# The attention-value product of every first query half in float16, each operand in two parts

## The chip, the cores and the metric

The kernel runs on one core of a Trainium2 chip. Five engines work side by side, each through its own queue in order: PE (matrix products, with a separate row PEld for loading the stationary operand), DVE (vector), ACT (activation), POOL (general purpose) and SP (here a queue that only issues transfers; ACT issues some too). They wait for each other by semaphores. Operands lie in SBUF, 128 partitions wide; matrix products write to PSUM. The metric is the time of one execution on the device in microseconds (us), and the median over runs is compared.

## The reference, cut to what matters

The program is one layer of gated attention and a feed-forward part, for four sequences of 512 tokens and 512 channels. The attention has a self branch and a cross branch; each has 8 groups of 2 query heads that share one key head and one value head, all 128 wide.

```python
ln_out = _ln(hidden_states, ln_w, ln_b)
q = _ln(_fp8_linear_pertensor(ln_out, wq, ...).reshape(b, s, g, hpg, d), qln_w, qln_b)
k = _ln(_fp8_linear_pertensor(ln_out, wk, ...).reshape(b, s, g, d), kln_w, kln_b)
v = _fp8_linear_pertensor(ln_out, wv, ...).reshape(b, s, g, d)
scores = jnp.einsum('bsghd,btgd->bghst', q, k) / np.sqrt(d)
core = jnp.einsum('bghst,btgd->bsghd', jax.nn.softmax(scores, axis=-1), v)
...
# the same once more with keys and values from ctx_2048 (no fp8 there): xout
catq = _div_clamp_fp8(jnp.concatenate([core, xout], axis=-1), proj_smooth)
out = jnp.einsum('bsi,oi->bso', catq, wproj) * (proj_in_scale * proj_w_scale)
```

`_div_clamp_fp8` rounds to 8-bit floating point, so a small error ahead of it can move a value by a whole step. That is why the products ahead of it are carried with more than 16 bits: either in float32, or as sums of float16 products, where a number x is held as a high part (x rounded to float16) and a low part (x minus the high part, rounded again). The feed-forward part after it (ternary weights, activations rounded to 8 bits) is not touched by the change.

## The kernel before, in words

**Tiling.** A block is one (branch, group, sequence): 64 blocks, first the 32 of the self branch, then the 32 of the cross branch. A block has two heads, and so two units of work; the main loop makes one step per unit, 128 steps. A unit's 512 queries are done in two halves of 256, h = 0 and h = 1. `half(n)` numbers all halves through, n = 2s + h for step s. The loop is followed by a stage that projects the attention's result and by the feed-forward stage.

**One half on PE.** `step` (line 805) is written as two passes, h = 0 and h = 1, and in each of them PE gets, in this order:

- `scores` of half n: 8 products of 256 columns into the PSUM tile `ps_s` (2 buffers)
- `shift_mm` of half n-1: 4 products of 256 columns, which subtract each query's largest score
- `pv` of half n-2 (line 668): the attention-value product, tile `po`, one buffer. 8 products of float32, 128 x 128 with 129 columns (the 129th column is of ones and yields the softmax's denominator). The page counts two PE records for each of them, 16 per half
- `top_turn` of half n: 2 small transposes of the running maxima into `mt`
- `mm` of a later block's token tile: the projections to queries, keys and values, tile `ps_p`, one buffer for each of the two token tiles of a pair. In the self branch 8 products of 256 columns and 16 of 128; in the cross branch 20 of 256
- `shift_row` of half n: 2 small products that lay the maxima out in a row, again `mt`

**Around it.** DVE makes `top` (tile `mx`, the maximum over `ps_s`), then for the projected tile of two halves ago `out` (line 564: `y`, `yj` with an accumulator, and `z`, the key's last step), `var`'s first half (line 554, tile `ss`, 128 x 3), then `nm` (the maximum over `mt`), and `evac` (line 682: the reciprocal `r` and two multiplications `ob`). ACT copies the row of maxima into `qk` (`shift_put`), writes `z` for the two query heads, squares the projected tile with a sum (`jk`), takes the exponential `pt` (line 665, 128 x 1024 float32) and copies the values to `vv`. POOL does `var`'s power, 128 x 3, which ends with the reciprocal square root.

**Once a step, in the pass h = 0.** `split` (line 579) makes the float16 parts of the queries and keys of a pair of token tiles: POOL adds a column to `z` (line 581), ACT casts the high part `hl` (128 x 768), POOL casts one more part (line 585) and subtracts for the low part (line 586), and SP issues a transposing transfer to `qk`. `quant` (line 694) rounds a unit's output to 8 bits on DVE in three passes over `ob`, 128 x 512; then SP issues a transposing transfer to `ot`, and ACT stores the `ot` of the unit before to DRAM, `cat_d`.

**In the background.** The weights of later groups are prepared piecemeal (`prep_w`, line 450: a sum `ms` and three multiplications `wf` on DVE, a cast `wq` on ACT and its low part on DVE, or POOL for some groups), as are the tokens of later sequences (`prep_self`, line 321) and the cross branch's context. A plan says at which point of which step each piece is put into the queues.

**What sets the order.** Instructions on PE, DVE and ACT go through `Ordered` (line 74). Where its switch is on, the order in the text is kept; elsewhere a scheduler orders them when the program is built. It is on from step 19 (`"p0"`, line 60) to three steps before the loop's end. POOL's and SP's instructions are not held to the text's order.

## Time and profile before

| what | value |
|---|---|
| median of 3 runs (lowest to highest) | 1761.45 us (1759.91 to 1762.43) |
| the profiled execution's own time | 1761.26 us |
| its span, first to last instruction | 1759.5 us |
| mean granted PE clock | 0.985 |
| busy share of the span | PE 95%, DVE 75%, ACT 60%, POOL 32% |
| start of the maxima in step 0 and step 19 | 61.9 us and 324.1 us |
| from one step to the next, steps 20 to 52 | 10.17 to 10.18 us |
| from one step to the next, steps 61 to 122 | 11.01 us |

The span is what lies between the first and the last instruction; the execution's own time is 1.8 us longer. Busy time is given for each engine; an engine can be busy all the time and still not be at its best rate, since the ends of PE's products are modelled. "Idle before" is what an engine waited ahead of an instruction, with the releaser that ended it. The chain that ended last is read backwards from the end: at each step to what released an instruction, or to its predecessor on its engine. A view in order of time gives start, duration, engine, line, operation and tiles (output first). Line 86 is the line in `Ordered` through which most instructions go, so here groups are told apart by tiles.

### The profile page before, as it was taken

Reading aid. Unit: us, or ns where it says so; the run is one execution under the profiler, and the core shown is the slowest. Engines: PE = TensorE matmul, PEld = TensorE weight load, DVE = VectorE, ACT = ScalarE, POOL = GpSimd, SP = SyncE. Lnnn points to the kernel's source line nnn. Section 1 sums busy time; section 2 is a strip of 40 time slices with the busy share of each in tenths; the row PEclk is TensorE's granted clock in tenths of the full one; section 3 lists DMA queues with packets and bytes.
Section 4 is the critical chain, followed back from the end, with each engine's and each line's share of the span. In section 5 each row is a group of like instructions: output and inputs, shape, how many; then the busy total and the mean of one; then the engine's idle time right before and its main releaser. Section 6 shows DMA issues by size and latency. Waiting matters only on the chain.

```text
span 1759.5 us, 40972 instructions
## 1 busy us (share of the span) xinstructions
PE 1672.0 (95%) x15174; PEld 1422.4 (81%) x15174; DVE 1324.2 (75%) x3967; ACT 1052.5 (60%) x3413; POOL 569.0 (32%) x725
## 2 busy tenths in 40 slices
PE   3589888999999999999999999999999999999999
PEld 2478787999999999999999999999999987443444
DVE  7888877777777778777777777777766665679876
ACT  6655555666666667666666666666665553457443
POOL 3453333334444335543333333333333330110000
PEclk8699999999999999999999999999999999999999
DMA  4433434344544455644445544544476664984333
GB/s 149 118 67 67 85 68 86 67 89 83 97 86 83 87 91 136 142 85 103 103 103 103 109 103 109 103 109 103 91 127 115 138 130 134 290 251 114 84 72 90
DMA packets 450312, 192.25 MB, mean 109 GB/s; under 512 B 417312, under 2 KB 421440, under 8 KB 447680
## 3 DMA queue, kind: packets, MB, share of 16 engines
q1 hardware_dynamic: 366688, 141.38, 38.7%
q10 hardware_dynamic: 82992, 44.07, 9.2%
q0 software_dynamic: 432, 4.19, 1.3%
q8 instruction: 119, 1.95, 0.4%
q14 instruction: 81, 0.66, 0.1%
HBM read 84.71 MB, written 23.09 MB: 61 GB/s over the span
## 4 chain that ended last, share of the span: by engine, by line
PE 82%; DVE 9%; ACT 3%; POOL 2%; DMA 2%; issue 1%; ACTq 0%; SPq 0%; DVEq 0%; POOLq 0%
PE ps_p L86 26%; PE po L86 23%; PE ps_s L86 17%; PE psj L86 5%; PE psd L86 3%; PE mt L86 3%; PE ub L86 3%; PE ga L86 3%; DVE mx L86 1%; DVE yb L86 1%; POOL ss L559 1%; DVE ob L86 1%; ACT z L86 1%; DMA ot<-ob 1%; DVE z L86 1%
## 5 line engine op out<-in xcount | busy, mean ns | idle before, releaser
L86 PE MATMUL ps_p<-wq,xa 128*128 128x256 f16 (+1 forms) x5584 | 557.5, 256 | 21.1 <-DVE xa L86 9.5
L86 PEld LDWEIGHTS <-xa 128*128 128x128 f16 x5632 | 471.7, 99 | 65.4 <-DVE xa L86 12.1
L86 PE MATMUL po<-vv,pt 128*128 128x129 f32 x4096 | 501.9, 275 | 0.0
L86 DVE TENSOR_REDUCE mx<-ps_s 128x256 f16<-128x1024 f32 x256 | 313.2, 1224 | 246.3 <-PE ps_s L86 244.9
L86 PEld LDWEIGHTS po<-vv,pt 128*128 128x128 f32 x4096 | 478.5, 192 | 4.0 <-PE ps_s L86 0.7
L86 PE MATMUL ps_s<-qk 128*128 128x256 f16 x3072 | 386.1, 274 | 14.8 <-ACT qk L86 8.0
L559 POOL TENSOR_TENSOR ss<-ss,mhalf 128x3 f32<-128x3 f32 x256 | 221.2, 864 | 497.2 <-DVE ss L86 490.1
L86 ACT CAST qk<-mt 1x256 f16<-1x256 f32 x256 | 92.4, 361 | 431.1 <-PE mt L86 422.0
L86 PEld LDWEIGHTS <-qk 128*128 128x128 f16 x3072 | 291.0, 98 | 49.1 <-issue 10.5
L86 ACT ACTIVATE pt<-ps_s 128x1024 f32<-128x1024 f32 x256 | 256.4, 1001 | 21.0 <-PE ps_s L86 20.3
L586 POOL TENSOR_TENSOR hl<-z,hl 128x768 f16<-128x768 f32 x126 | 207.4, 1646 | 19.6 <-ACT hl L86 19.6
L86 ACT ACTIVATE jk<-ps_p 128x128 f32<-128x128 f32 x762 | 192.3, 253 | 22.5 <-PE ps_p L86 19.1
L86 ACT ACTIVATE z<-ps_p,ss 128x127 f32<-128x127 f32 x508 | 154.4, 350 | 51.3 <-POOL ss L559 51.1
L86 DVE SCALAR_TENSOR_TENSOR ob<-po,r,rsr 128x128 bf16<-128x128 f32 x512 | 155.9, 346 | 7.7
L86 ACT ACTIVATION_READ_ACCUMULATOR jk<-ps_p 128x1 f32 x762 | 142.9, 188 | 0.0
L581 POOL TENSOR_TENSOR z<-acc,cb 128x2 f32<-128x2 f32 x128 | 27.2, 213 | 337.0 <-DVE ss L86 293.3
L86 DVE TENSOR_REDUCE nm<-mt 128x2 f16<-128x256 f16 x256 | 107.4, 419 | 29.4 <-PE mt L86 29.3
L86 DVE TENSOR_SCALAR ob<-ob 128x512 bf16<-128x512 bf16 (+2 forms) x384 | 111.9, 291 | 8.3
L86 ACT CAST hl<-z 128x768 f16<-128x768 f32 x128 | 105.8, 827 | 19.3 <-POOL z L581 17.1
L86 DVE SCALAR_TENSOR_TENSOR y<-ps_p,ss,gk 128x128 f32<-128x128 f32 x254 | 87.1, 343 | 28.8 <-ACT z L86 27.9
L86 PEld LDWEIGHTS <-nt 128*128 128x128 bf16 x512 | 50.0, 98 | 65.4 <-issue 6.2
L86 PE MATMUL psj<-wp,cat 128*128 128x512 f16 x448 | 97.0, 379 | 0.0
(149 smaller groups left out, 1773.8 us busy)
## 6 DMA issues: line engine op xcount, KB each, us to landing
cat_d<-ot ACTq DMA_DIRECT2D x128, 128.0 KB, 2.0
cat<-cat_d SPq DMA_DIRECT2D x16, 1024.0 KB, 5.6
wf<-in_dram ACTq DMA_DIRECT2D x56, 256.0 KB, 4.3
wt<-in_dram ACTq DMA_DIRECT2D x48, 256.0 KB, 4.3
wt<-in_dram SPq DMA_DIRECT2D x24, 512.0 KB, 4.4
xt<-in_dram SPq DMA_DIRECT2D x32, 256.0 KB, 4.4
cf<-in_dram SPq DMA_DIRECT2D x16, 256.0 KB, 3.6
out_dram<-o SPq DMA_DIRECT2D x16, 256.0 KB, 2.0
```

What stands on the lines that cost most here:

```text
L86: ins = f(*args, **kw)
L559: gp.tensor_tensor(ss[:, 2], ss[:, 1], mhalf[:, 0], ALU.pow)
L581: gp.tensor_tensor(z[:, :, 2, 0:1], self.acc, cb[:, self.ty : self.ty + 1].broadcast_to((128, 2, 1)), ALU.add)
L586: (low or gp).tensor_tensor(hl[:, :, 3:6], z, hl[:, :, 0:3], ALU.subtract)
```

## The change

- **The product.** For h = 0, `exps` writes the exponentials to a float32 tile `e` (one buffer). A new `high` on ACT casts it to float16 into the first half of the place where `pt` was, and a new `low` on DVE writes `e` minus that, in float16, into the second half. `pv` then takes three float16 products (high x high, high x low, low x high) in place of each float32 product: 24 products of 129 columns in place of 8. For h = 1 nothing is changed in the product but a bias in the exponential; `pt` and `vv` stay float32.
- **The values.** `vals` scales by 1/8; a new `vals16`, once a step, makes the two float16 parts of the values on POOL: a cast and a subtraction, 128 x 256 each.
- **The key's last step.** DVE's third instruction in `out` goes. A new `keys`, once a step, does it on POOL: a copy of one column, two instructions of 128 x 256 (subtract that column, add `hk`), and then the two small POOL instructions that `split` had. The rest of `split` becomes `high` and `low` of the pair.
- **The variance.** Its first half moves from DVE to POOL, two POOL instructions in place of one on each engine; a factor goes into constants.
- **The output's rounding.** `ob` belongs to a block, so `quant` runs once in two steps over 128 x 1024; one transposing transfer of twice the size in place of two, and two stores one step later. `quant` now stands at the end of the pass h = 0, behind `evac`.
- **Order.** POOL's instructions go through `Ordered` too, the switch is on from step 16, one background point moves from the end of a step to the middle of its pass h = 1, the weights' pieces come at three yields in four, and the scale tile `rsr` is loaded in 8 parts, not 4.

```diff
-    "p0": 19,
+    "p0": 16,
...
-    v, sc, pe = [Ordered(tc, e) for e in (nc.vector, nc.scalar, nc.tensor)]
-    gp, sy = nc.gpsimd, nc.sync
+    v, sc, pe, gp = [Ordered(tc, e) for e in (nc.vector, nc.scalar, nc.tensor, nc.gpsimd)]
+    sy = nc.sync
...
             def var(self, i):
                 ss = self.ss[:, i]
-                v.scalar_tensor_tensor(
-                    ss[:, 1], ss[:, 0], 1.0 / 128, epsv[:, self.ty, 0], ALU.mult, ALU.add
+                gp.tensor_tensor(ss[:, 1], ss[:, 0], epsv[:, self.ty], ALU.add)
+                gp.tensor_tensor(ss[:, 2], ss[:, 1], mhalf[:, 0], ALU.pow)
+
+            def vals(self, i):
+                sc.activation(
+                    self.v[:, self.pr * 2 + i, 0:128], self.ps[i][:, 384:512], AF.Copy, scale=V_SCALE
                 )
-                gp.tensor_tensor(ss[:, 2], ss[:, 1], mhalf[:, 0], ALU.pow)
-
-            def vals(self, i):
-                sc.copy(self.v[:, self.pr * 2 + i, 0:128], self.ps[i][:, 384:512])
+
+            def vals16(self):
+                tk = slice(self.pr * 2, self.pr * 2 + 2)
+                v32, vh, vl = self.v[:, tk, 0:128], self.v16[:, 0, tk, 0:128], self.v16[:, 1, tk, 0:128]
+                gp.tensor_copy(vh, v32)
+                gp.tensor_tensor(vl, v32, vh, ALU.subtract)
...
-                v.scalar_tensor_tensor(y, k, r[:, 2:3], gk[:, ty], ALU.mult, ALU.mult)
+                v.scalar_tensor_tensor(z[:, 2], k, r[:, 2:3], gk[:, ty], ALU.mult, ALU.mult)
...
-                v.scalar_tensor_tensor(z[:, 2], y, y[:, 0:1], hk[:, ty], ALU.subtract, ALU.add)
-
-            def split(self, low=None):
+
+            def keys(self):
                 z, hl = self.z, hl_tiles[self.k % 2]
+                k, y0 = z[:, :, 2], sm.tile([128, 2, 1], F32, name="y0", bufs=2)
+                gp.tensor_copy(y0, z[:, :, 2, 0:1])
+                gp.tensor_tensor(k, k, y0.broadcast_to((128, 2, 128)), ALU.subtract)
+                gp.tensor_tensor(k, k, hk[:, self.ty : self.ty + 1].broadcast_to((128, 2, 128)), ALU.add)
                 gp.tensor_tensor(
                     z[:, :, 2, 0:1], self.acc, cb[:, self.ty : self.ty + 1].broadcast_to((128, 2, 1)), ALU.add
                 )
-                sc.copy(hl[:, :, 0:3], z)
                 gp.tensor_copy(hl[:, :, 6, 1:128], z[:, :, 2, 1:128])
+
+            def high(self):
+                sc.copy(hl_tiles[self.k % 2][:, :, 0:3], self.z)
...
             def exps(self, h):
-                sc.activation(self.pt[:, h], self.ps.pop(h), AF.Exp)
+                if h:
+                    sc.activation(self.pt[:, h], self.ps.pop(h), AF.Exp, bias=pbias)
+                    return
+                self.e = ep.tile([128, NT, 256], F32, name="e", tag="e", bufs=1)
+                sc.activation(self.e, self.ps.pop(h), AF.Exp, bias=pbias)
+                self.p16 = self.pt[:, h].rearrange("p t q -> p (t q)").bitcast(F16).rearrange(
+                    "p (a t q) -> p a t q", a=2, t=NT
+                )
+
+            def high(self):
+                sc.copy(self.p16[:, 0], self.e)
+
+            def low(self):
+                v.tensor_tensor(self.p16[:, 1], self.e, self.p16[:, 0], ALU.subtract)
...
+                        if h:
+                            terms = [(pt[:, h, t, i * 128 : i * 128 + 128], vv[:, t, 0:129])]
+                        else:
+                            terms = [
+                                (self.p16[:, a, t, i * 128 : i * 128 + 128], v16[:, b, t, 0:129])
+                                for a, b in ((0, 0), (0, 1), (1, 0))
+                            ]
...
             def quant(self):
-                ob = self.ob
+                ob = self.blk.ob
...
+                if w3 and not w3[1]:
+                    w3[0].vals16()
...
+                if h:
+                    background(5 * s + 4 + LEAD)
+                if w2 and w2[1]:
+                    w2[0].keys()
+                if w3 and w3[1]:
+                    w3[0].high()
+                    w3[0].low()
+                if u1 and not h1:
+                    u1.high()
                 if q:
                     q.mm((h,))
                     tiles[0].append((q, h))
-                if w3 and w3[1]:
-                    w3[0].split()
-                if h == 0 and u3:
-                    run(u3.quant())
-                    u3.turn_out()
-                    turned.append(units.pop((n - 3) // 2))
-                    if len(turned) > 1:
-                        turned.pop(0).store()
                 if u0:
                     u0.shift(h0)
                     u0.shift_row()
                 if u2:
                     run(u2.evac(h2))
+                if u1 and not h1:
+                    u1.low()
+                if h == 0 and u3:
+                    units.pop((n - 3) // 2)
+                    if u3.j:
+                        run(u3.quant())
+                        u3.turn_out()
+                        turned.append(u3)
+                    elif turned:
+                        turned.pop().store()
                 background(5 * s + 1 + 2 * h + LEAD)
-            background(5 * s + 4 + LEAD)
```

## The prediction

> **What bounds the kernel now.** I read first the page's chain and its groups, then the busy time by stretches, the chain of two stretches, and one step in order of time.
>
> ```profile
> PE 82%; DVE 9%; ACT 3%; POOL 2%; DMA 2%; issue 1%; ACTq 0%; SPq 0%; DVEq 0%; POOLq 0%
> ```
> ```profile
> 150.00:200.00 50.00, 44.65 (x465) 40.53 (x463) 44.98 (x120) 27.79 (x95) 17.03 (x20) 1.00 0.43 88
> 400.00:500.00 100.00, 100.00 (x1097) 95.52 (x1096) 77.23 (x252) 64.48 (x239) 41.94 (x54) 1.00 0.50 91
> 900.00:1000.00 100.00, 100.00 (x948) 93.35 (x946) 74.63 (x239) 64.39 (x235) 35.14 (x46) 1.00 0.51 104
> ```
> ```profile
> by line: DVE mx L86 9.0%; POOL ss L559 8.1%; DVE ob L86 6.8%; DVE yb L86 6.7%; issue 5.7%; PE ps_p L86 5.4%; PE ps_s L86 4.9%; ACT z L86 4.4%; DMA ot<-ob 4.1%; DVE z L86 3.7%; PE po L86 3.6%; ACT jk L86 3.3%; DVE ss L86 3.1%; ACT hl L86 2.8
> ...
> by line: PE ps_p L86 38.0%; PE po L86 33.4%; PE ps_s L86 24.5%; PE mt L86 4.2%
> ```
> The stretches give busy us of PE, PEld, DVE, ACT and POOL, then the granted clock. From about 325 us to 1430 us PE never idles at full clock, and the chain of 400 to 1400 us is PE alone: 104 steps (40 self, 64 cross) whose length is PE's sum of work. The other chain is that of 60 to 324 us, the first 19 steps, which take 13.8 us each where PE needs 10.2: a chain through DVE, POOL and ACT, with PE's three largest rows at 14%.
>
> One half of the self branch in order of time (start, duration, engine; the half begins with `ps_s` at 404.46 and ends 5.09 us later):
>
> ```profile
> 404.46 1.47 PE L86 MATMUL ps_s<-qk 128*128 128x256 f16 x12
> ...
> 405.54 1.23 DVE L86 TENSOR_REDUCE mx<-ps_s 128x256 f16<-128x1024 f32 x1
> ...
> 405.77 1.95 PE L86 MATMUL po<-vv,pt 128*128 128x129 f32 x16
> ...
> 407.20 0.08 DVE L86 DVE_READ_ACCUMULATOR yj<-ps_p,ss,ck 128x1 f32 x1
> ...
> 407.24 0.83 ACT L86 CAST hl<-z 128x768 f16<-128x768 f32 x1
> ...
> 407.56 0.28 PE L86 MATMUL mt<-ident,mx 128*128 128x128 f16 x2
> ...
> 407.67 1.93 PE L86 MATMUL ps_p<-wq,xa 128*128 128x256 f16 x24
> ...
> 409.44 0.28 PE L86 MATMUL mt<-ident,nm 128*128 128x128 f16 x2
> ```
> See that `po` keeps PE from 405.77 to 407.56, 1.79 us, and that DVE is done with `yj`, the last reader of the projection's PSUM tile, at 407.28, 0.39 us before the projection (407.67) needs it. That 0.39 us is the cover the change draws on.
>
> The last view shows DVE and POOL in each other's way:
>
> ```profile
> 181.85 1.64 POOL L586 TENSOR_TENSOR hl<-z,hl 128x768 f16<-128x768 f32 x1 [2.38 <-ACT hl L86]
> ...
> 182.16 1.36 DVE L86 SCALAR_TENSOR_TENSOR ss<-ss,epsv 128x3 f32<-128x3 f32 x1
> ```
> A DVE instruction on 3 elements, 0.15 us at other times, lasts until POOL's subtraction has ended at 183.49. In another place a DVE pass over 16-bit data (`xa`, 0.63 us as a rule) takes 1.89 us beside the same POOL instruction, and the DVE pass ahead of it stretches that POOL instruction from 1.64 to 2.12 us. DVE's `mx`, `ob`, `y` and `yj` have the same length with and without POOL.
>
> **The change part by part.** Durations are those of the profiled execution of 1761.26 us (0.2 us under the median); the sum is made against it.
>
> *The product, on PE.* Float16 products of 128 columns with their own weights are in the self projections: 24 products from 407.67 to 409.44 are 1.77 us; 8 of 256 columns at 0.109 us (12 `ps_s` in 1.31 us) are 0.87, so 16 of 128 columns take 0.90, 0.056 us each. 24 of 129 columns: 1.35 us. PE saves 1.79 - 1.35 = 0.44 us a step.
>
> *What is late next.* Counted from the half's start, the half h = 0 now has its product from 1.31 to 2.66 and could start the projection at 2.77. `yj` is done at 2.82 (407.28 - 404.46), 2.88 with the semaphore: 0.11 us wait. Net gain 0.33 us a step, 34 us over 104 steps, if nothing else is late.
>
> *High and low part of the exponentials.* ACT's cast of 1024: 0.83 us for 768, 0.61 for 512, so 1.04; ACT is 64% busy and runs it after `vv` in h = 1, done at about 4.0 to 4.4. DVE's subtraction of 1024 lies between 1.22 (`mx` reads as many) and 1.36 (twice 0.68, `wq` with 512); I take 1.22. DVE's queue in h = 1: `mx` 1.08 to 2.31, `yj` to 2.82, a weight piece (0.7 to 0.9), `nm`, `r` and `ob` to about 4.6, then the subtraction to 5.9, or 0.8 in the next half. Its reader, the third product there, starts at 1.42; `mx`, queued behind it, is due at 1.08. Covered, by 0.3 us for `mx`.
>
> *Taken from DVE.* Two `z` (0.27 each as spaced), two `ss` (0.07 to 0.15), and a quarter us of rounding per step: DVE's sum per step stays within 0.2 us of before.
>
> *Added to POOL, per step.* Two additions of 3 elements at 0.20 (as line 581), two instructions of 128 x 256 for the keys (0.61 to 0.74 us in the constants' rows; I take 0.70), a column copy (0.18), for the values a cast (0.40, as line 585) and a subtraction (0.70): 3.1 us on 4.0 us in 9.8 us. POOL does not become the bound, but is now on its two-input instructions for some 60% of a step, and in the text's order.
>
> *The rounding, once in two steps.* A pass of 1024: 512 take 0.29 and 2048 take 0.68 to 0.79, so 0.42, three of them 1.3. It now stands behind `evac` in h = 0: `nm` 2.98, `r` 3.32, `ob` 3.5, ready at 4.06. POOL's `low` of the pair starts when ACT's `hl` ends (407.24 + 0.83, so 3.61 from the half's start), hence at 3.67, and runs 1.64 us, to 5.3. By the rows above the rounding's first pass waits for that, and its later ones alternate with POOL's value cast and subtraction (0.40 and 0.70), which follow at once: the third ends at about 6.9. Behind it stands the next half's `mx`, due at 4.76 + 1.08 = 5.84: 1.0 us late. `yj` ends 1.74 us after `mx` starts, at 8.6; the projection of that half was due at 4.76 + 3.21 = 7.97. PE waits 0.7 us in every second step. In the cross branch the projections are 0.41 us longer (20 x 0.109 against 1.77), so the next half begins at 5.17 and its projection is due at 8.38: 0.2 to 0.3 us wait; I take 0.3.
>
> The Trainium skill, page SBUF — State Buffer, section Who interferes with whom, says that a DVE instruction with two SBUF inputs, or one in a two-port fast mode, and a POOL instruction that reads SBUF exclude each other for a whole instruction. It speaks against this change, which fills POOL with such instructions; the rows above agree (1.36 us against 0.15). Without that exclusion for the rounding the cross steps would win about 0.1 us each, an estimate of 6 us on the sum; the forecast takes the row.
>
> *Sum of the loop's 104 steps.* Self: 2 x 0.33 - 0.7 = -0.04 for two steps, so 40 x 0.02 = +1 us. Cross: (2 x 0.33 - 0.3) / 2 = 0.18, so 64 x 0.18 = -11 us. Ends: -34 (no collision) and +10 (POOL's 256 at 0.80 and no slack: 0.15 us a step in self, 0.05 in cross).
>
> *The first 19 steps.* Not PE's, and before step 16 the scheduler orders them. Lower end: PE's 0.44 each, -8 us. Upper end: DVE busy 80% there (210 of 264 us), each step taking DVE's 0.14 net plus one exclusion of 1.1 us (as the rounding's first pass): 19 x 1.24 = +24. Also POOL's `ss`, 8% of that chain, stands behind more POOL work. PE is the smaller part of that chain, so it lies above the middle between gain and nothing; I take 0.25 a step, +5.
>
> *Beginning and end.* The constants lose an ACT instruction and gain two short DVE ones; eight loads of half the size replace four; the last four steps have no projection, and the longer path from exponential to product there (1.04 + 1.22) lies in a gap of 4.1 us (`pt` ends at 1480.1, its product starts at 1484.2). Half as many transposing transfers go through SP's queue, and the wait for them is on DVE's `ob`, two steps ahead. Zero, between -3 and +3.
>
> Sum: 1 - 11 + 5 = -5; 1761 - 5 = **1756 us**. A measurement tells about 0.2% (3.5 us) from no change.
>
> **The rivals.**
>
> - *No collision costs PE anything* (chance 0.20). The weight pieces and POOL's `low` fall apart in time, and only the 0.11 us stays. For it: the `wq` subtractions in the trace stand right behind POOL's power in nearly every step and keep 0.68 us. Against it: the 0.39 us between POOL's `low` and the rounding is the same in every second step. 1761 - 34 = 1727, to 1732 with the opening's 5.
> - *The opening grows* (0.20), the rival on the other side. Place: the first 19 steps; mechanism: DVE's subtraction and rounding wait for POOL's instructions, and POOL's power behind them. For it: DVE is at 45 us of 50 between 150 and 200 us, and the 1.36 us above is from there. Against it: some ten such waits of before go with `ss` and `z`. Price at the upper end: 1761 + 24 - 10 = 1775. It decides from 0.5 us a step, where it eats the cross steps' 10 us.
> - *`mx` of h = 0 is late in every step* (0.12). DVE's subtraction, caught by half a POOL instruction of 0.70, ends 0.35 later, against 0.05 to 0.3 of spare: about 0.3 x 104 = 31, so 1787 from the forecast's 1756. It decides from 0.05 us a step.
> - *The float16 products don't run at 0.056* (0.03). A weight load shows as 98 ns; at that rate 24 take 2.35 us, 0.56 more than before, 128 x 0.56 = +72: 1833. Against it: the 16 products of 128 columns above load as many weights.
>
> **How the numbers follow.** The forecast has 0.42, 1748 to 1768 by its own terms (0.26 of it faster by over 0.2%, 0.12 within, 0.04 slower); 0.03 is left for nothing I named, as slower. Faster: 0.26 + 0.20 = 0.46. Within: 0.12, and 0.02 from a small growth of the opening. Slower: 0.04 + 0.18 + 0.12 + 0.03 + 0.03, with rounding 0.40. The range leaves out 0.06 above, and the lower part of the first rival: 1727 to 1787.
>
> **What would show each step.** `po` should have 3072 records of 128x129 f16 and half the float32 ones, a product of h = 0 taking 1.35 us. Cross steps about 10.8 us, self steps 10.2, in turn shorter and longer. PE's waits should name DVE `yj` and `mx`; SP's and DMA's should not grow. POOL's busy share should be near 55%, `ss` and the subtraction `pt<-e,pt` of more than 1.3 us where POOL overlaps. Step 19 should come near 329 us. The prediction is wrong if steps of both branches are near 9.85 and 10.67 (first rival), if step 19 comes after 340 us (second), or if PE waits for `mx` in h = 0 (third).

## The result, and the profile after

| | before | after |
|---|---|---|
| median of 4 runs (lowest to highest) | 1760.84 us (1759.91 to 1762.43) | 1790.08 us (1789.24 to 1790.89) |
| ratio, with its 95% interval | | 1.0165 (1.0147 to 1.0183) |
| the profiled execution's own time; its span | 1761.26 us; 1759.5 us | 1790.89 us; 1789.1 us |
| mean granted PE clock | 0.985 | 0.975 |
| busy share PE, DVE, ACT, POOL | 95, 75, 60, 32% | 93, 84, 67, 59% |
| steps of the self branch | 10.18 us | 9.98 and 10.54 us in turn |
| steps of the cross branch | 11.01 us | 10.69 and 11.07 us in turn; the long ones 11.67 to 11.98 between steps 79 and 104 |

The change made the kernel slower by 29 us, 1.65%. The forecast was 1756 us with a range of 1727 to 1787.

The page's chain after the change:

```profile
PE 64%; DVE 19%; ACT 5%; issue 4%; POOL 4%; DMA 2%; ACTq 0%; SPq 0%; POOLq 0%; DVEq 0%
```

PE fell from 82% to 64% of the chain, DVE rose from 9% to 19%. The same three stretches as before (busy us of PE, PEld, DVE, ACT, POOL, then the granted clock):

```profile
150.00:200.00 50.00, 41.61 (x435) 36.63 (x432) 37.24 (x83) 28.86 (x88) 25.47 (x44) 0.93 0.24 50
400.00:500.00 100.00, 97.97 (x1168) 90.69 (x1165) 92.09 (x204) 74.16 (x247) 79.80 (x121) 1.00 0.46 90
900.00:1000.00 100.00, 98.75 (x1036) 90.38 (x1034) 90.97 (x201) 76.15 (x249) 69.11 (x110) 1.00 0.54 107
```

PE idles now in both steady stretches (98 and 98.8 of 100 us), and DVE is at 91 to 92. In the opening DVE has come down (37 of 50 us against 45), PE too (41.6 against 44.7), and the clock, 0.93 against 1.00; POOL does more there (25 against 17). The chain of the opening, and below it the chain of 400 to 1400 us:

```profile
by line: PE ps_p L89 11.7%; PE po L89 10.3%; PE ps_s L89 7.9%; POOL z L89 7.7%; POOL ss L89 7.5%; issue 6.9%; POOL hl L89 4.0%; ACT pt L89 4.0%; ACT jk L89 3.6%; DMA wf<-in_dram 2.4%; DVE mx L89 2.4%; DVE pt L89 2.3%; ACT yb L89 2.3%; DVE o
...
by line: PE ps_p L89 30.0%; PE po L89 19.9%; PE ps_s L89 17.2%; DVE ob L89 11.9%; DVE mx L89 5.5%; issue 4.6%; PE mt L89 3.1%; DVE yj L89 1.3%; DVE z L89 1.2%; DMA ot<-ob 1.0%; DVE r L89 0.7%; ACT jk L89 0.6%; ACT z L89 0.6%; ACT qk L89 0.4
```

In the opening POOL's `z`, most of it the keys' last step, which was DVE's before, holds 7.7%, and POOL's `hl` 4.0%; DVE's `mx`, first before with 9.0%, has 2.4%. PE's three largest rows have gone from 14% to 30%, in part at half the clock (see the last section). In the steady steps `ob` (the rounding, for the most part) holds 11.9% and `mx` 5.5% of a chain that had been PE alone. Two stages, two different engines.

One step of the self branch in order of time (start, duration, engine):

```profile
507.99 1.44 DVE L89 TENSOR_TENSOR pt<-e,pt 128x1024 f16<-128x1024 f32 x1
...
509.48 1.53 PE L89 MATMUL po<-vh,pt 128*128 128x129 f16 x24
...
511.01 0.08 DVE L89 DVE_READ_ACCUMULATOR yj<-ps_p,ss,ck 128x1 f32 x1
...
511.15 1.94 PE L89 MATMUL ps_p<-wq,xa 128*128 128x256 f16 x24
...
511.94 1.65 POOL L89 TENSOR_TENSOR hl<-z,hl 128x768 f16<-128x768 f32 x1 [0.74 <-ACT hl L89]
512.22 3.00 DVE L89 TENSOR_SCALAR ob<-ob 128x1024 bf16<-128x1024 bf16 x3
...
513.53 0.59 POOL L89 CAST vh<-vv 128x256 f16<-128x256 f32 x1
...
514.21 0.73 POOL L89 TENSOR_TENSOR vh<-vv,vh 128x256 f16<-128x256 f32 x1
...
515.14 1.21 DVE L89 TENSOR_REDUCE mx<-ps_s 128x256 f16<-128x1024 f32 x1
...
516.94 1.94 PE L89 MATMUL ps_p<-wq,xa 128*128 128x256 f16 x24 [0.24 <-DVE yj L89]
```

The float16 product takes 1.37 us to the next product (509.48 to 510.85), and the projection behind it waits for `yj`, as worked out. Then the rounding, three passes, starts 0.28 us behind POOL's subtraction, ends after POOL's two instructions for the values, and has taken 3.00 us, where the prediction had estimated 1.3 for the passes alone. `mx` stands behind it and PE behind `mx`. PE's waits between 400 and 1430 us (what waited for what: us in total, times, longest):

```profile
PE ps_p L89 <- DVE yj L89: 10.1, 44, 0.2
PE mt L89 <- DVE mx L89: 8.2, 19, 0.7
```

Where the 29.9 us came from can be read off the start of the maxima (`mx`) in chosen steps. Difference from before, us, each from one trace (the traced execution of the first experiment below took 6185 us where its three others took 1793, so only these three times are used of it):

| kernel | step 4 | 19 | 59 | 79 | 104 | 127 |
|---|---|---|---|---|---|---|
| after | +12.1 | +21.1 | +25.3 | +23.9 | +30.7 | +29.9 |
| product alone | +0.7 | +3.6 | +49.0 | +61.2 | +78.1 | +76.7 |
| keys on DVE | +3.1 | -2.8 | -0.3 | -3.1 | +4.3 | +0.1 |
| POOL's subtraction cut | +5.9 | +11.3 | +5.5 | -0.4 | -7.1 | -12.7 |
| POOL's order free | +8.9 | +17.7 | +14.7 | +11.2 | +14.5 | +12.5 |
| opening as before | +7.0 | +3.6 | +7.3 | +5.8 | +12.6 | +11.6 |
| order from step 19 | +9.1 | +20.9 | +25.2 | +23.7 | +30.5 | +29.3 |
| rounding at its old place | +9.4 | +19.9 | +27.5 | +21.6 | +13.9 | +6.4 |
| keys on POOL alone | +6.7 | +12.4 | +12.2 | +12.4 | +12.4 | +15.1 |

So 21 us of the 30 are lost before step 19, 4 in the self steps after it, 5 in the cross branch (7 of loss between steps 79 and 104, small gains around that). What makes the steps between 79 and 104 long is seen in one of them, of 11.98 us:

```profile
1068.02 1.64 POOL L89 TENSOR_TENSOR hl<-z,hl 128x768 f16<-128x768 f32 x1 [0.74 <-ACT hl L89]
1068.30 3.00 DVE L89 TENSOR_SCALAR ob<-ob 128x1024 bf16<-128x1024 bf16 x3
...
1071.21 0.54 DVE L89 TENSOR_REDUCE ms<-wf 128x3 f32<-128x384 f32 x1
...
1071.87 1.22 DVE L89 TENSOR_REDUCE mx<-ps_s 128x256 f16<-128x1024 f32 x1
...
1073.14 0.28 PE L89 MATMUL mt<-ident,mx 128*128 128x128 f16 x2 [0.43 <-DVE mx L89]
```

Behind the rounding, which is as late as in the other long steps, stands an instruction of a weight piece, and only then `mx`. It is `ms` here; in the others it is `wq` (0.68 us) or the three passes `wf` (0.33 each). `mx` starts 6.50 to 6.67 us after the step's first maxima, in the steps of 11.07 us 5.89.

### The profile page after: what moved, and what is told of

Its sections match the earlier page's. It is cut to its first block, busy times and chain, and to the rows that moved or that the text cites. A ratio compares the mean times of both kernels' runs of the same rounds, so it can differ in the third digit from the quotient of the medians.

```text
span 1789.1 us, 43329 instructions
## 1 busy us (share of the span) xinstructions
PE 1660.9 (93%) x16198; PEld 1379.7 (77%) x16198; DVE 1502.5 (84%) x3389; ACT 1195.3 (67%) x3540; POOL 1051.7 (59%) x1628
## 4 chain that ended last, share of the span: by engine, by line
PE 64%; DVE 19%; ACT 5%; issue 4%; POOL 4%; DMA 2%; ACTq 0%; SPq 0%; POOLq 0%; DVEq 0%
PE ps_p L89 21%; PE po L89 15%; PE ps_s L89 13%; DVE ob L89 8%; DVE mx L89 4%; PE psj L89 4%; PE psd L89 3%; PE ub L89 3%; PE ga L89 3%; PE mt L89 2%; POOL ss L89 1%; POOL z L89 1%; DVE z L89 1%; DVE yj L89 1%; ACT jk L89 1%
## 5 line engine op out<-in xcount | busy, mean ns | idle before, releaser
L89 PE MATMUL po<-vv,pt 128*128 128x129 f32 x2048 | 256.5, 278 | 0.0
L89 PEld LDWEIGHTS po<-vv,pt 128*128 128x128 f32 x2048 | 244.5, 195 | 2.6 <-PE ps_s L89 0.7
L89 PE MATMUL po<-vh,pt 128*128 128x129 f16 x3072 | 199.0, 220 | 4.2 <-DVE pt L89 3.4
L89 PEld LDWEIGHTS <-pt 128*128 128x128 f16 x3072 | 186.7, 97 | 9.3 <-DVE pt L89 4.7
L89 POOL TENSOR_TENSOR ss<-ss,epsv 128x3 f32<-128x3 f32 x256 | 59.6, 233 | 214.6 <-ACT jk L89 213.7
L89 DVE TENSOR_SCALAR ob<-ob 128x1024 bf16<-128x1024 bf16 (+2 forms) x192 | 172.4, 898 | 4.0
L89 DVE TENSOR_TENSOR pt<-e,pt 128x1024 f16<-128x1024 f32 x128 | 172.7, 1349 | 2.4 <-ACT pt L89 2.0
L89 ACT ACTIVATE pt<-ps_s,pbias 128x1024 f32<-128x1024 f32 x128 | 139.9, 1093 | 14.7 <-PE ps_s L89 14.7
L89 ACT ACTIVATE e<-ps_s,pbias 128x1024 f32<-128x1024 f32 x128 | 140.0, 1094 | 8.1 <-PE ps_s L89 8.0
L89 ACT CAST pt<-e 128x1024 f16<-128x1024 f32 x128 | 132.2, 1033 | 0.3
```

The costliest lines, as they stand in the source:

```text
L89: ins = f(*args, **kw)
```

## The experiments

Each measured time is a median, with its ratio to the kernel before on the same chip and the 95% interval. Edits are against the changed kernel unless another is named; `...` stands for lines not shown.

### The product: taken out, and alone

```diff
-                if h:
+                if h or not (False):
                     sc.activation(self.pt[:, h], self.ps.pop(h), AF.Exp, bias=pbias)
                     return
...
-                        if h:
+                        if h or not (False):
                             terms = [(pt[:, h, t, i * 128 : i * 128 + 128], vv[:, t, 0:129])]
```

(with `high`, `low` and `vals16` not issued)

> The changed kernel with the product of h = 0 back in float32: no cast and no subtraction of the exponentials, no float16 values; keys on POOL, variance on POOL, rounding once per block and POOL's fixed order stay. Theory A (the product itself pays, and the parts moved to POOL cost the time): the opening stays late (step 19 within 6 us of the changed kernel's 345), self steps 10.2 as there, cross steps 11.0 as in the kernel before, so 1790 to 1800 us. Rival B (the product's cast and subtraction on ACT and DVE cost the time): it comes back to 1760 to 1765 us, or below.

Measured: 1793.49 us, 1.0187 (1.0170 to 1.0204). Theory A's time held; what its steps took is not shown. Inside the changed kernel the float16 product is worth about 3 us, where PE's saving by itself is 46 (104 x 0.44).

The reverse, the kernel before with the product alone:

```diff
+                            terms = [
+                                (self.p16[:, a, t, i * 128 : i * 128 + 128], v16[:, b, t, 0:129])
+                                for a, b in ((0, 0), (0, 1), (1, 0))
+                            ]
...
+                if w3 and not w3[1]:
+                    w3[0].vals16()
...
+                if u1 and not h1:
+                    u1.low()
```

> The kernel before with the float16 product alone: cast on ACT, subtraction on DVE behind the evacuation, values' parts on POOL; the key's last step and the variance stay on DVE, the rounding once a unit at its old place, POOL free of the text's order. Theory A (DVE's queue is then too long for PE's shorter step: the wait before the projection and the late maxima are what the other parts of the change were bought for): steps of 10.8 us or more in self and cross, 1790 us or more. Rival B (the product is a gain of 0.33 us a step by itself, the other parts lose it): 1725 to 1745 us.

Measured: 1835.65 us, 1.0428 (1.0413 to 1.0444). A held, by more than its bound. The self steps take 11.29 us on average (steps 20 to 40). One of its halves in order of time:

```profile
509.41 1.69 POOL L606 TENSOR_TENSOR hl<-z,hl 128x768 f16<-128x768 f32 x1
509.53 1.59 DVE L89 SCALAR_TENSOR_TENSOR ss<-ss,epsv 128x3 f32<-128x3 f32 x1
511.04 0.94 DVE L89 TENSOR_SCALAR ob<-ob 128x512 bf16<-128x512 bf16 x3
...
511.89 0.42 DVE L89 TENSOR_REDUCE nm<-mt 128x2 f16<-128x256 f16 x1
...
512.37 0.28 PE L89 MATMUL mt<-ident,nm 128*128 128x128 f16 x2 [1.29 <-DVE nm L89]
```

PE's waits in this kernel between 400 and 1430 us:

```profile
PE mt L89 <- DVE nm L89: 47.1, 56, 1.3
PE mt L89 <- DVE mx L89: 12.7, 23, 1.1
```

With the longer way DVE runs late enough to meet POOL's subtraction with an instruction on 3 elements, which then takes 1.59 us in place of 0.15; rounding and `nm` queue behind it, and PE waits 1.29 us. From step 108 on, when no weight pieces are left for DVE, the steps of this kernel take 10.69 us (to step 122): the stall goes with them. So what the change does along with the product is not idle: without it the product costs 75 us, with it the whole costs 29.

### The opening: keys, order, or the step from which order holds

Keys' last step back on DVE, for all pairs:

```diff
-                v.scalar_tensor_tensor(z[:, 2], k, r[:, 2:3], gk[:, ty], ALU.mult, ALU.mult)
+                y = zp.tile([128, 128], F32, name="y", tag="y", bufs=1)
+                v.scalar_tensor_tensor(y, k, r[:, 2:3], gk[:, ty], ALU.mult, ALU.mult)
...
+                v.scalar_tensor_tensor(z[:, 2], y, y[:, 0:1], hk[:, ty], ALU.subtract, ALU.add)
```

> The changed kernel with the key's last step back on DVE (two multiplications more a step there, three instructions fewer on POOL). Theory A (POOL's longer work stands in the opening's chain): step 0 starts 3 to 5 us earlier than the changed kernel's 71.6, step 19 5 to 12 us earlier; in the loop self 10.3 to 10.4, cross about 10.8; in all 1775 to 1788 us. Rival B (DVE bounds the opening): the opening grows by another 5 us and the whole to 1795 us or more.

Measured: 1758.93 us, 0.9992 (0.9982 to 1.0001): all of the loss is gone, more than any theory gave it. By the table 24 of the 30 us come back before step 19, and the rest between steps 104 and 127 and in small pieces. Step 0 is no mark of it: theory A had its maxima at 67 to 69 us, they start at 77.1, later than the changed kernel's 71.6, and by step 4 this kernel is 9 us ahead of that one. Does the gain sit in the opening alone?

```diff
-                gp.tensor_tensor(ss[:, 1], ss[:, 0], epsv[:, self.ty], ALU.add)
+                (v if self.k < 24 else gp).tensor_tensor(ss[:, 1], ss[:, 0], epsv[:, self.ty], ALU.add)
...
+                on_dve = self.k < 24
```

> The changed kernel, but for the first 24 pairs of tiles (those that feed the beginning and steps 0 to 19) the keys' last step and the variance's addition are on DVE as before; later pairs as changed. Theory P: the opening's loss goes as with the keys on DVE throughout (24 us at step 19), the rest stays: 1762 to 1770, step 19 within 3 us of before. Rival O (order of POOL, which stays fixed here): 1782 to 1790. Rival S (the keys on POOL cost mostly in the steady steps): 1780 to 1790.

Measured: 1772.47 us, 1.0069 (1.0054 to 1.0084). P's direction held in the opening: step 19 is 3.6 us behind, not 21.1, so 17.5 us come back, where P had 24 and a step 19 within 3 us. The median is 2.5 us above P's range; from step 19 on the kernel loses 8.0 us, as the changed one does (8.8).

```diff
-    v, sc, pe, gp = [Ordered(tc, e) for e in (nc.vector, nc.scalar, nc.tensor, nc.gpsimd)]
+    v, sc, pe = [Ordered(tc, e) for e in (nc.vector, nc.scalar, nc.tensor)]
+    gp, sy = nc.gpsimd, nc.sync
```

> The changed kernel, with POOL's instructions left to the scheduler instead of being issued in the text's order; everything else is as changed. After: 1790 us, of which the beginning (to the first step's maxima) holds 9.7 us and steps 0 to 19 another 11.4. Theory P (POOL's additional work, above all the keys' last step, is late whatever its order): 1783 to 1793, step 19 still 15 us or more behind before. Rival O (it is POOL's fixed order that puts the keys behind weight pieces and variance behind keys): the beginning and the opening come back, 1765 to 1778, step 19 within 8 us of before.

Measured: 1774.57 us, 1.0083 (1.0068 to 1.0098). The median is in O's range, but not for O's reason: step 19 is still 17.7 us behind, as P said. POOL's order costs 3.4 us up to step 19 (6.1 at step 0, 65.5 against 71.6 us) and 14 from there to step 127; the long steps fall to 10.20 and 10.73 us: the scheduler puts POOL's two instructions for the values ahead of the subtraction, so the rounding meets the subtraction alone and takes 2.67 us, not 3.00.

```diff
-    "p0": 16,
+    "p0": 19,
```

> The changed kernel, with the text's order beginning at step 19 as before, not at step 16. Theory P: the three steps don't matter, 1786 to 1794. Rival T (steps 16 to 18, where the written order begins too early, cost part of the 11.4 us of the opening): 1780 to 1786.

Measured: 1791.01 us, 1.0179 (1.0162 to 1.0196). P held; those three steps are nothing.

The keys by themselves: of the change, their last step on POOL stays, and the smaller parts (constants, the scale tile's loads, the weights' pieces, the place of the casts in a step, order from step 16).

```diff
-    v, sc, pe, gp = [Ordered(tc, e) for e in (nc.vector, nc.scalar, nc.tensor, nc.gpsimd)]
+    v, sc, pe = [Ordered(tc, e) for e in (nc.vector, nc.scalar, nc.tensor)]
...
-                gp.tensor_tensor(ss[:, 1], ss[:, 0], epsv[:, self.ty], ALU.add)
+                (v).tensor_tensor(ss[:, 1], ss[:, 0], epsv[:, self.ty], ALU.add)
...
-                if h:
+                if h or not (False):
```

> Nearly the kernel before: float32 products throughout, variance's addition on DVE, rounding per unit at its old place, POOL's order left to the scheduler; only the keys' last step is on POOL (and the constants of the change stay). Theory K (the keys' place on POOL alone holds the opening's loss): step 19 at 8 to 20 us behind before, steady steps as before (10.18 and 11.01), 1769 to 1781. Rival X (the opening's loss comes from the longer way from exponential to product, or from the fixed order of POOL): step 19 within 4 us of before, 1758 to 1765.

Measured: 1777.49 us, 1.0098 (1.0081 to 1.0115). K held: 12.4 us at step 19, and then within 0.3 us the same until step 104; another 3 us come in the loop's last steps. That it is the keys and not the smaller parts is told by the run with the product in the cross branch alone (below): up to there it is this kernel with the keys on DVE, and its step 19 is 0.2 us behind. So the keys' place costs 12.2 us, nearly all of it between steps 4 (6.7 against 5.7) and 19. The steady steps don't notice the move; the opening does. What it does there can be seen at the start of the first pair, here in the kernel before:

```profile
46.10 0.34 DVE L86 SCALAR_TENSOR_TENSOR z<-y,hk 128x128 f32<-128x128 f32 x1
...
46.51 0.20 POOL L581 TENSOR_TENSOR z<-acc,cb 128x2 f32<-128x2 f32 x1 [1.02 <-DVE ss L86]
...
46.75 0.83 ACT L86 CAST hl<-z 128x768 f16<-128x768 f32 x1 [0.99 <-POOL z L581]
```

and here in the changed kernel:

```profile
48.36 0.95 POOL L89 TENSOR_TENSOR ss<-ss,mhalf 128x3 f32<-128x3 f32 x1
...
49.46 0.85 POOL L89 TENSOR_TENSOR ss<-ss,mhalf 128x3 f32<-128x3 f32 x1
50.26 0.19 POOL L89 COPY y<-z 128x2 f32<-128x2 f32 x1
50.53 0.61 POOL L89 TENSOR_TENSOR z<-z,y 128x256 f32<-128x256 f32 x1
51.22 0.72 POOL L89 TENSOR_TENSOR z<-z,hk 128x256 f32<-128x256 f32 x1
52.02 0.20 POOL L89 TENSOR_TENSOR z<-acc,cb 128x2 f32<-128x2 f32 x1
...
52.25 0.83 ACT L89 CAST hl<-z 128x768 f16<-128x768 f32 x1 [3.17 <-POOL z L89]
```

ACT's cast of the high part needs the keys. Before, it came 0.31 us after DVE's pass. After, POOL first does the next tile's variance and power (48.1 to 50.3), then 1.8 us of keys, and the cast comes at 52.25. The chain to the first scores goes on through the second pair's keys (60.97 to 62.90), which stand behind a weight piece on POOL (58.84), and through the transfer to `qk` (65.22, 4.91 us). The steady steps did not get longer by such waits (10.18 and 11.01 us in the run with the keys alone).

### The steady steps: rounding and POOL's subtraction

```diff
+            v.memset(t[:, :, 3:6], 0.0)
...
+                c = slice(0, 2)
-                (low or gp).tensor_tensor(hl[:, :, 3:6], z, hl[:, :, 0:3], ALU.subtract)
+                (low or gp).tensor_tensor(hl[:, :, 3:6, c], z[:, :, :, c], hl[:, :, 0:3, c], ALU.subtract)
```

> The changed kernel with POOL's subtraction for the low part of queries and keys cut from 128 x 768 to 128 x 12; the rest of the low part is left out, so only the time of that one instruction (1.65 us a step) is taken away, and no wait is. Theory A (the rounding and DVE's other passes wait for exactly this instruction): the three rounding passes fall from 3.0 us to 1.3 to 1.9, self steps to 10.0 to 10.2, cross steps to 10.7, 10 to 25 us less than the changed kernel. Rival B (DVE is simply full): the passes get shorter but the steps stay within 0.05 us.

Measured: 1749.16 us, 0.9934 (0.9919 to 0.9949), 41 us less than the changed kernel, 10 of it by step 19 and the rest after. The direction of A held, its size was too small; the three passes together take 1.84 us, within A's 1.3 to 1.9. PE's waits for `mx` and `yj` are gone. The passes of the rounding between 400 and 500 us (minimum/median/maximum in ns) in the changed kernel:

```profile
L89 DVE TENSOR_SCALAR ob<-ob x15: 499/780/1649, 409.7 to 493.9; 128x1024 bf16<-128x1024 bf16 x5, 128x1024 f16<-128x1024 bf16 x5, 128x1024 uint16<-128x1024 uint16 x5
```

and in this one:

```profile
L89 DVE TENSOR_SCALAR ob<-ob x16: 426/564/782, 399.7 to 499.2; 128x1024 f16<-128x1024 bf16 x6, 128x1024 uint16<-128x1024 uint16 x5, 128x1024 bf16<-128x1024 bf16 x5
```

Nothing of the rounding was changed here, only the POOL instruction beside it; the passes are shorter for that. (POOL's queue is shorter by 1.6 us a step too, and what that alone gains is not told apart here.) Moving the rounding and leaving the subtraction is the other side:

```diff
+                if h == 0 and u3:
+                    run(u3.quant())
+                    u3.turn_out()
...
                 if u0:
                     u0.shift(h0)
                     u0.shift_row()
...
-                    if u3.j:
-                        run(u3.quant())
```

> The changed kernel, with the output's rounding done once per unit at its old place (three passes of 512 ahead of nm, not three of 1024 behind evac); everything else as changed. Theory R (in the steady steps the rounding stands behind POOL's subtraction and is what makes every second step long): the steps of 10.54 and 11.07 us fall to 9.9 to 10.2 and 10.69 to 10.75, the opening stays 18 to 24 us behind: 20 x 0.4 + 32 x 0.35 = 19 us less than after, 1765 to 1776. Rival C (some DVE instruction or other waits for POOL's subtraction wherever the rounding stands): steps keep 10.4 and 11.0, 1785 to 1795.

Measured: 1766.44 us, 1.0034 (1.0022 to 1.0045). R's number held, and its steps in the cross branch (10.67 to 10.73, all of them from step 66 on); from step 59 to 127 the kernel is 21.1 us faster than before, where the changed one is 4.6 slower. In the self branch R held in steps 27 to 42 (9.85 and 10.05) but not in the others (10.29 and 10.84): there something else is late.

The sum of both repairs:

```diff
+                on_dve = self.k < 24
...
+                if h == 0 and u3:
+                    run(u3.quant())
+                    u3.turn_out()
```

> The changed kernel (1790.1) with two parts undone together: the keys' last step on DVE for the first 24 pairs, and the rounding once per unit at its old place. Theory Sum (the opening's loss and the steady steps' loss are two separate things): the rounding alone gave -23.7 (1766.4), and the opening of the run with the variance's addition and the keys on DVE for those pairs 17.5 at step 19: 1746 to 1752. Rival V (in the opening DVE is full, and rounding per unit makes three passes more of it): 1756 to 1764.

Measured: 1742.84 us, 0.9903 (0.9888 to 0.9918), 3 us below the sum's range: the two losses are separate and add up. The sum had taken 17.5 us for the opening from a run that has the variance on DVE there; here it is on POOL, and step 19 is 2.1 us ahead of before, 23 us better than the changed kernel's. Its self steps are in turn 9.84 and 10.05 in steps 27 to 42 and 10.29 and 10.83 around them, as in the run before. In a long one the trace shows:

```profile
614.06 0.89 DVE L89 TENSOR_TENSOR wq<-wf,wq 128x512 f16<-128x512 f32 x1 [0.69 <-ACT wq L89]
...
614.87 0.41 DVE L89 TENSOR_REDUCE nm<-mt 128x2 f16<-128x256 f16 x1
...
615.92 1.31 DVE L89 TENSOR_TENSOR pt<-e,pt 128x1024 f16<-128x1024 f32 x1
...
618.81 2.38 DVE L89 TENSOR_SCALAR ob<-ob 128x512 bf16<-128x512 bf16 x3
...
619.40 1.64 POOL L89 TENSOR_TENSOR hl<-z,hl 128x768 f16<-128x768 f32 x1 [0.73 <-ACT hl L89]
...
621.58 0.29 PE L89 MATMUL mt<-ident,nm 128*128 128x128 f16 x2 [0.70 <-DVE nm L89]
```

and at about the same place in the next run, which has this weight piece on POOL:

```profile
608.25 0.42 DVE L89 TENSOR_REDUCE nm<-mt 128x2 f16<-128x256 f16 x1 [0.59 <-PE mt L89]
608.40 1.16 POOL L89 TENSOR_TENSOR wq<-wf,wq 128x512 f16<-128x512 f32 x1 [0.53 <-ACT wq L89]
...
609.31 1.33 DVE L89 TENSOR_TENSOR pt<-e,pt 128x1024 f16<-128x1024 f32 x1
...
612.67 0.95 DVE L89 TENSOR_SCALAR ob<-ob 128x512 bf16<-128x512 bf16 x3
```

A weight piece `wq` on DVE makes `nm` late by 0.9 us (it starts 0.31 us after `mt` in the second list, 1.23 after it in the first, where `mt` is at 613.64), the low part of the exponentials with it, and then the rounding, which meets POOL's subtraction after all (2.38 us). Where `wq` is on POOL the rounding is through (0.95 us) in time. Counted from the start of the half's scores (`ps_s`, 615.63 and 609.93) the rounding starts 0.44 us earlier there, and the subtraction 0.28 us later. The edit:

```diff
-    "l3": "---pvppv",
+    "l3": "---ppppp",
```

> As the run with the keys of the first 24 pairs on DVE and the rounding per unit at its old place (1742.8), with the low part of the weights (wq) of all self groups from the third on subtracted on POOL; there, two of these groups are on DVE. In that run the self steps take 9.84 and 10.05 where wq is on POOL (1.16 us a piece) and 10.29 and 10.83 where it is on DVE (0.89 us, ahead of nm and the low part of the exponentials). Theory Q (the DVE piece is what makes them long): steps 20 to 26 and 43 to 52 go to 9.95 on average, 0.6 us x 17 = 10 us less, 1731 to 1737. Rival H (POOL's longer piece delays its other work by as much): 1740 to 1748.

Measured: 1735.85 us, 0.9858 (0.9841 to 0.9874). Q held: steps 20 to 49 take 9.84 to 10.06. What is left of long self steps lies in 51 to 58.

```diff
+            gp.on[0] = Ordered.on[0] and not 50 <= s < 60
```

> As the run before it in this list, with POOL's order left to the scheduler in steps 50 to 59, where POOL also works on the cross branch's inputs (xa, 1.2 us a piece) and the rounding behind it takes 2.4 to 3.3 us, nm coming 1.6 us late. Theory U (in another order these pieces don't meet the rounding): steps 55 to 58 fall from 10.3 to 12.1 us to 10.0 to 10.5, 4 us less than the run before it. Rival J (they meet it, or the maxima, all the same): within 2 us of it.

Measured: 1733.74 us, 0.9847 (0.9833 to 0.9862), 2.1 us less than the run beside it. Between the two theories and nearer to J: steps 56 and 57 fall from 12.1 to 9.8 and 10.5 us, but steps 50 to 52 take 11.1 to 11.5 instead. Whether it is the same collision, moved, is not shown. This is the fastest of all kernels here, 1.5% under the kernel before.

### The product in one branch

```diff
+                on_dve = self.ty == 0
...
-                if h:
+                if h or not (self.blk.ty == 1):
                     sc.activation(self.pt[:, h], self.ps.pop(h), AF.Exp, bias=pbias)
```

> The float16 product only in the cross branch's units; keys' last step on DVE in the self branch (the opening with it) and on POOL in the cross branch, variance's addition on DVE, rounding once per unit at its old place, POOL's order left to the scheduler. Theory P (POOL against DVE in the opening, and the rounding behind evac in the steady steps): self steps as before (10.18 us), cross steps 10.67 against 11.01, so 64 x 0.34 = 22 us less than before, less a few where weight pieces of the second branch collide: 1738 to 1750. Rival B (collisions just move, PE still waits for the maxima or yj): 1755 to 1770.

Measured: 1746.72 us, 0.9921 (0.9906 to 0.9936). P held: self steps 10.18, cross steps 10.68 to 10.73 from step 66 on, and nine of 11.16 from step 80 to 104. In such a step:

```profile
994.53 2.26 DVE L89 TENSOR_SCALAR wf<-wf,sw,ms 128x128 f32<-128x128 f32 x3
994.56 1.64 POOL L619 TENSOR_TENSOR hl<-z,hl 128x768 f16<-128x768 f32 x1
```

The three `wf` passes of a weight piece take 0.86 us when alone. In the changed kernel such a piece takes 2.55 us in the same stretch, but in steps of 10.72 us: there it starts earlier in the step, and `mx` behind it (5.45 us after the step's first maxima, 5.99 here) is late by less. Two attempts at these steps, the first against the kernel just measured (the number of pieces goes back too):

```diff
-        for s in range(n_steps - 47, n_steps - 22, 2):
+        for s in range(n_steps - 46, n_steps - 22, 4):
```

> As the run with the float16 product in the cross branch alone (1746.7), with the weight pieces of the change put back as before: two pieces of a group of four passes, not three, and fewer points. There, eight cross steps take 11.16 us where the others take 10.70. Theory W (the additional points put a weight piece beside POOL's subtraction): these steps go to 10.7, 1742 to 1744. Rival L (a longer piece at a point is late for the maxima just as well): 1746 to 1752.

Measured: 1753.32 us, 0.9954 (0.9939 to 0.9969). W fell; it went L's way, 1 us beyond its range. Three steps of 11.61 took the place of nine of 11.16, and every second self step came to 10.36. So in this order of work the finer pieces of the change pay. The second attempt, against the same kernel:

```diff
+            gp.on[0] = 60 <= s < n_steps - 3
...
-                (v).tensor_tensor(ss[:, 1], ss[:, 0], epsv[:, self.ty], ALU.add)
+                (v if self.ty == 0 else gp).tensor_tensor(ss[:, 1], ss[:, 0], epsv[:, self.ty], ALU.add)
```

> As the run with the float16 product in the cross branch alone (1746.7), but in the cross branch POOL's instructions are issued in the text's order and the variance's addition is on POOL. Theory N (order decides whether POOL's subtraction meets the weight piece, whose three passes then take 2.26 us and delay the maxima): the eight steps of 11.16 us go to 10.7 as in the run with the rounding alone put back, so 4 us less: 1740 to 1744. Rival G (the weight piece is there all the same and meets another POOL instruction): 1745 to 1749.

Measured: 1742.45 us, 0.9898 (0.9883 to 0.9913). N held: the long steps are gone (10.68 to 10.72 from step 66 on). The piece still meets the subtraction, but starts 0.9 us into it and takes 1.94 us, which the maxima can bear. POOL's fixed order, which costs 14 us from step 19 on with the rounding at its new place, gains 4 here with the rounding at its old place (and the variance on POOL; which of the two does it was not tried). Against this kernel, the product in the self branch too:

```diff
-                if h or not (self.blk.ty == 1):
+                if h:
                     sc.activation(self.pt[:, h], self.ps.pop(h), AF.Exp, bias=pbias)
```

> As the run before it in this list, with the float16 product in the self branch too (the keys' last step there stays on DVE). Theory P (the longer way from exponential to product fills DVE and meets POOL's subtraction, so the self branch does not gain): opening 3 to 8 us behind, self steps 10.1 to 10.4 on average: 1744 to 1754. Rival F (with the keys back on DVE the self branch gains too, steps of 9.9 to 10.0): 1730 to 1738.

Measured: 1761.05 us, 1.0006 (0.9996 to 1.0015), 7 us above P's range, 19 more than without the product in the self branch: 7.1 at step 19, 12.7 in the self steps (10.32 to 10.56). F fell. The next run differs in the self branch only in the keys of the pairs after the 24th, which are on POOL; its self steps are 10.20 us on average against 10.46 here, so with the low part of the exponentials on DVE the keys have a price there too.

```diff
+                on_dve = self.k < 24
...
+                (v).tensor_tensor(ss[:, 1], ss[:, 0], epsv[:, self.ty], ALU.add)
```

(against the changed kernel: product in all units, rounding at its old place, POOL's order free)

> The float16 product in every unit as changed; keys' last step on DVE for the first 24 pairs and on POOL after that, variance's addition on DVE, rounding per unit at its old place, POOL's order left to the scheduler. Beside the run with the float16 product in the cross branch alone (1746.7) it tells what the self branch makes of it. Theory P (self steps fall by what is left when the projection waits for yj and the maxima, 10.0 to 10.15 against 10.18, and the opening gives 0 to 5 us away): 1740 to 1750. Rival F (the first one of the prediction: nothing costs PE anything): self steps of 9.85, 1730 to 1738. Rival O (the longer way in the opening costs more than the self steps give): 1752 to 1760.

Measured: 1754.16 us, 0.9963 (0.9948 to 0.9977). The self steps alternate between 9.85 to 10.0 and 10.43 to 10.55, 10.2 on average, and the opening gives 7.4 away; O's range held. Against the sum of both repairs (1742.8) it has the variance on DVE and POOL's order free. By the start of the maxima that costs 9.5 us up to step 19 and 6 from step 59 on, and gains 5 between them.

The last one is against the kernel with the product in the cross branch alone:

```diff
-                on_dve = self.ty == 0
+                on_dve = True
```

> As the run with the float16 product in the cross branch alone (1746.7), with the keys' last step on DVE in the cross branch as well, so that there only the product is changed. The run with the product alone in all units had steps of 11.5 us, with nm 1.3 us late behind a 3-element DVE instruction that waited for POOL's subtraction. Theory M (moving the keys to POOL pays in the steady steps, by 0.7 us of DVE a pair, though it costs in the opening): cross steps 11.0 to 11.5, 1765 to 1795. Rival Z (the keys' place does not matter in the cross branch): 1743 to 1752.

Measured: 1752.89 us, 0.9958 (0.9943 to 0.9972). M fell and Z missed by 0.9 us: the keys on DVE cost 6 us against 1746.72, nearly all of it in steps 79 to 104 (11.23 and 11.27 in two of three). The stall of the product alone does not come back. This kernel keeps the order of work that the change gives to the casts, the subtraction and the weight pieces, and that one does not; which of these prevents the stall was not tried, but the stall of that one ends with its weight pieces.

## Why the prediction was wrong

Measured is 34 us more than forecast. By the start of the maxima, the beginning and the first 19 steps hold 16 of that (21.1 against 5), the self steps 3 (4.2 against 1), the cross steps 16 (+4.6 against -11). Two steps of the working failed: in the opening POOL's added work was given no price, and behind the late rounding `mx` was taken to come next, with no weight piece between them.

- **The product, 1.35 us.** Right (1.37). The projection's wait for `yj` comes as predicted, and the net 0.32 us a step (11.01 to 10.69) wherever nothing else is late; 0.33 had been worked out.
- **The collision of the rounding.** The mechanism and its place were right: POOL's subtraction, the rounding, the value parts, `mx`, PE. The size in the cross branch was taken as 0.3 us in every second step; measured 0.38. In the self branch 0.7 was taken, measured 10.54 - 9.98 = 0.56, but the short steps are 9.98, not 9.85. Pairs: self 10.26 against 10.20 predicted, cross 10.88 against 10.83. (Without the exclusion the cross steps would by the working's own terms win 0.15 us each, 10 us and not 6.)
- **The cross branch, "-11".** It came to +4.6. Of that difference 3 us are the 0.05 just named over 64 steps. The main term was missing: in steps 79 to 104 every second step takes 11.67 to 11.98 us, 0.75 more than 11.07 on average, thirteen times, 10 us. (Single long steps hold the rest.) The failing step is "Behind it stands the next half's `mx`": in these steps `ms`, `wq` or `wf` of a weight piece stands between the rounding and `mx`, and the rounding has used up what `mx` could wait. The working had a weight piece in the half h = 1 alone. With the rounding at its old place and the same pieces these steps take 10.67 to 10.73.
- **DVE's sum, "within 0.2 us of before".** It was 77 of 100 us before, is 92 after, and still 90 with POOL's subtraction cut, so waiting for POOL is not all of it. What else was not taken apart.
- **The first 19 steps, "+5".** +11.4, and with the beginning's +9.7 the rival "the opening grows" is what happened: its sign, its mark (step 19 after 340 us; it came at 345.25) and, roughly, its price of 24. Its mechanism was not, or in its last clause alone. It said that DVE would wait for POOL, and POOL's power behind that; but DVE's rows on that chain shrank, the power's did not grow (`ss` 8.1% before, 7.5% after), and POOL's own added instructions stand on it. The keys' place alone is worth 12.2 us at step 19. Keys on DVE for the opening's pairs take 17.5 of the 21.1 us away when the variance goes back with them, and 23 or 24 when it stays on POOL: so there the variance's move gained some 6 us.
- **The beginning, "zero, between -3 and +3".** +9.7. It counted constants, loads and the last steps, and none of POOL's added work, which was priced by the sum of busy time (3.1 us on 4.0 in 9.8) and not by who waits for its last instruction. The working said that POOL "does not become the bound", which is true of a steady step and beside the point in the opening. How much of the 9.7 is whose is less clear: 6.1 go when POOL's order is left to the scheduler. The other 3.6 are also there with keys and variance on DVE and POOL's order free (4.2 in the run with the product in the cross branch alone), so they belong to neither; where they come from stays open.
- **POOL in the text's order** was named and given no price. It costs 15.5 us (1790.1 to 1774.6), most of it as a larger rounding collision (0.34 us in every second step of both branches).

What stays open: keys on DVE in all pairs gain 13.5 us more than in the opening's pairs alone. Some 6 of these are the variance before step 19 (the run with two parts undone, with the keys of 24 pairs on DVE and the variance on POOL, has its step 19 where the run with all keys on DVE has it). 5 come between steps 19 and 127 (2.9 lost, not 8.0), where the two kernels differ in the later pairs' keys alone. Why these gain there, while the keys by themselves did not change the steady steps of float32 products, no run shows.

## What to carry to other kernels

Price moved work by the instruction that waits for its result, stage by stage: a move that costs a steady step nothing cost the opening 12 us here, where that very result stood on the chain. Where two engines block each other, a list of all instructions of the blocked kind is needed, with all that stands behind each; the same POOL subtraction met the rounding, the weight pieces and an instruction on three elements in turn, and the dearest steps were those where the late rounding had one more instruction behind it, ahead of `mx`. And a part of a change that looks like a loss may be what the rest stands on: the product alone cost 75 us, the whole 29, and the whole with the opening's keys, the rounding and one kind of weight piece put elsewhere gained 25 to 27.

## What the runs showed of the hardware

- Waiting is not a matter of size. DVE's addition of 3 elements took 1.59 us beside POOL's subtraction, three passes of 128 x 128 in float32 took 2.26 and 2.55 us (0.86 alone), while `mx`, a reduction from PSUM, kept 1.21 to 1.23 in every row shown, and 1.23 at 611.00 us of the run with the weight pieces on POOL, beside two POOL instructions of 128 x 256. The Trainium skill, page SBUF — State Buffer, section Who interferes with whom, counts instructions with two SBUF inputs among those that contend with POOL's reads, `tensor_scalar` passes among those that can, and reductions (`tensor_reduce`) not. The rows agree, for 32-bit passes as for 16-bit ones (the rounding took 3.00 us, and 1.84 with the subtraction cut).
- When three DVE passes and three POOL instructions meet, they take turns: the rounding ended only after all of POOL's three (515.22 against 514.94 us). With two of these moved ahead it was 0.33 us shorter.
- Gaps of PE in the opening came with a lower clock. The granted clock of 72 to 150 us fell from 0.89 to 0.79, and single groups took twice their time: 24 projection products 3.43 us at 80.16, where the granted clock is 0.50, after a gap of 3.10 us before 79.07; the 16 records of `po` 3.42 us at 187.28 (0.52) after a gap of 2.17 us before 186.19. At full clock they take 1.77 and 1.79.
- The exponential of 128 x 1024 took 1.09 us with a bias tile and 1.00 without.
